# Softplus in a selective scan: the maximum and the exponential in one VectorE sum, the bias as a row of the weights, eight z buffers and seven weight buffers

## The chip, the cores and the metric

The kernel runs on one core of one Trainium2 chip. The metric is the device time of one execution in microseconds (us), as the median over several runs. All arithmetic is float32.

Engines are named as in the profile: PE is TensorE (PEld its weight loads), DVE is VectorE, ACT is ScalarE, POOL is GpSimd, SP is the queue of SyncE, which here starts nearly all DMAs. SBUF is the on-chip working memory, PSUM the accumulator memory that PE writes and that DVE and ACT can also use for other data.

## The reference, cut to what matters

The input is four images of 384 channels by 32 by 32 pixels (1024 positions). Layer 0 is a group norm followed by a selective scan in four directions, summed, normalised and passed through a GELU. Layer 1 is windowed attention over tokens and then a mixture of four experts, two per token. The change touches the time step `dt` of the scan only:

```
xs    = _cross_scan(x)                                     # 4 directions k, 384 channels d, 1024 positions l
x_dbl = einsum('bkdl,kcd->bkcl', xs, x_proj_weight)        # 44 rows: 12 for dt, 16 for B, 16 for C
dts   = einsum('bkrl,kdr->bkdl', x_dbl[:, :, :12], dt_projs_weight)
dt    = softplus(dts + dt_projs_bias[None, :, :, None])
# scan, for each of 16 states per channel:
h     = h * exp(dt * A) + (dt * u) * B
y     = sum over the states of h * C
```

So two things leave the softplus: `dt` itself, which feeds the exponentials, and the product `dt * u`, which feeds the other factor.

## The kernel before, in words

**Tiling.** A turn is one image and one direction; there are 16. A turn has three channel tiles of 128, so there are 48 time steps in the sense of `time_steps` (L741): one computes `dt` and `dt * u` for 128 channels and 1024 positions. Each time step then serves 16 scan slots: a tile of 128 partitions holds 32 channels times 4 states, so 4 blocks of channels times 4 groups of states, 768 slots in all.

**One time step** (L741 to L796). PE multiplies 12 rows of `x_dbl` (tile `xd`) by the weights `dtw_sb` into two PSUM banks of 512 positions each (`ps_dt`). ACT takes the absolute value into `e` and the ReLU into `dt`, adding the bias in both, and gives the banks back. ACT makes `e = exp(-e)` over 1024 positions. It takes two banks again (`ps_sp`, called `w` in the code), writes `w = 1 + e`; DVE computes the rounding error `e = (w - 1) - e`, ACT takes the logarithm of `w` in place, and DVE, for each half, subtracts `e`, adds `dt` (both into `w` in PSUM), and multiplies `w` by the input `u` (tile `ub`) into `e` in SBUF. ACT copies `w` into `dt` in SBUF and the bank goes back. Two DMAs write `e` and `dt` to DRAM (`dtr`), from where `spread` (L798) loads them repeated four times per channel (tiles `dtu` and `dts`).

**One slot.** POOL multiplies the spread `dt * u` by B into a z buffer (`times_b`, L808). ACT makes `dA = exp(dt * A)` in PSUM, in one of two `dA` tiles (`decay`, L824). DVE runs the recurrence (`scan`, L850) either in place in z or into `dA`. The product with C follows on POOL (`z<-z,bc`) or on DVE (`z<-dA,bc`), whichever the planner finds earlier free. PE sums the four states of each channel (`fold_y`, L884), one PSUM bank for eight slots, and then gives the z buffers back.

**Buffers.** There are `NZ = 7` z buffers of 4 KB per partition, and `NWT = 8` buffers of 4.5 KB (`wt`) for expert weights; while the attention of an image runs, four of these hold its weights. Three PSUM banks are shared by the folds, the softplus and all other work (`banks`), and one more serves the experts' output.

**What sets the order.** The kernel is written as generators, one per task. At build time `Machine.run` (L335) steps them against a table of costs (`Engine.ask`, L154) and fixes the order of the instructions of every engine: at each step the engine that can start first issues its earliest ready request, with a bias for early or late tasks. On the chip every engine and the SP queue run this order strictly in turn, each waiting for what its next instruction needs. A bank or a buffer is taken in the planner, and on the chip its next writer waits for its last reader.

**Stages.** Group norm and projection of the first image fill the first 100 us. The scan of all four images follows, with attention, routing and experts of the earlier images in the gaps. When the last slot is done, attention of the last image and the rest of the experts remain (`experts`, L1317: 19 blocks of 128 tokens per image, 76 in all). A block uses eight weight tiles, four of the first layer (`ps_hid`) and four of the second (`y_ff`).

**Start of the SP queue.** Constants are loaded first (L394 to L405, `const_load`), among them the bias `dtb_sb`; the next instruction in the queue, the first load of `x`, waits for the set-up work on DVE.

Of the kernel before, what the change touches and what calls it, by code (L numbers as in the profile page):

```python
# [11 lines left out]
F32 = mybir.dt.float32  # L12
AF = mybir.ActivationFunctionType
ALU = mybir.AluOpType
# [3 lines left out]
P = 128  # L18
B, D, HH, WW = 4, 384, 32, 32
L = HH * WW  # L20
T = D // P
HB = 512
NH = L // HB
KG, NS, R = 4, 16, 12
# [12 lines left out]
NCH, HT = HID // CH, CH // P  # L37
MB = 2 * L // P + NE - 1
NT = L // P
NROW, NHS, NWT = 10, 4, 8  # L40
EARLY, LATER = -6.0, 6.0
LEAD = 0.6
HID_RANK = 2
GELU_BIAS = EARLY
FAVOUR = 1.0
TILES, EPS, NZ = 3, 1e-5, 7
CORES = 1
NEG = -1.0e30

# [17 lines left out]
def colmajor(ap):  # L67

    return ap.rearrange("p (h w) -> p w h", w=WW)
# [307 lines left out]
def conv_attn_hybrid(  # L377
# [7 lines left out]
    nc = tc.nc  # L385
    const = ctx.enter_context(tc.tile_pool(name="const", bufs=1))
    dram = ctx.enter_context(tc.tile_pool(name="dram", bufs=2, space=bass.MemoryType.DRAM))

    def const_load(src, shape, name):
        dst = const.tile(shape, F32, name=name)  # L390
        nc.sync.dma_start(dst, src)
        return dst

    xw_sb = const_load(xw, [P, T, KG, XR], "xw_sb")  # L394
    dtb_sb = const_load(dtb, [P, KG, T], "dtb_sb")
    ds_sb = const_load(ds_, [P, KG, T], "ds_sb")
    lnw_sb = const_load(lnw, [P, T], "lnw_sb")
    lnb_sb = const_load(lnb, [P, T], "lnb_sb")
# [72 lines left out]
    banks = Stock(m, ps_b, "ps", 3, [P, HB])  # L471
# [4 lines left out]
    with tc.tile_pool(name="setup", bufs=1) as setup:  # L476
# [15 lines left out]
        for j in range(JB):  # L492
            ps = banks.now("ps_al")
# [15 lines left out]
    work = ctx.enter_context(tc.tile_pool(name="work", bufs=1))  # L509
# [42 lines left out]
    pe, act, dve, pool, sp = m.pe, m.act, m.dve, m.pool, m.sp  # L552
# [65 lines left out]
    def group_norm(b):  # L618
# [68 lines left out]
        def project(pair):  # L687
            xos = yield from zs_.take("xo", n=2)
            for h in range(NH):
                us = yield from us_.take("ux", n=2)  # L690
                uv = [us[t // NH][:, ts(t % NH, HB)] for t in range(T)]
                for t in range(T):
                    yield from sp.dma_start(uv[t], udr[b][t][:, ts(h, HB)])
                ps = yield from banks.take("ps_x", 0)
                pv = ps[: 2 * XR, :]
                mm = Calls()
                for t in range(T):
                    mm.matmul(
                        pv, xw_sb[:, t, 2 * pair : 2 * pair + 2, :].rearrange("p k r -> p (k r)"),
                        uv[t], start=t == 0, stop=t == T - 1,  # L700
                    )
                yield from pe.all(mm)
                us_.give(*us)
                yield from act.copy(xos[0][: 2 * XR, ts(h, HB)], pv)
                yield from copy(
                    xos[1][: 2 * XR, :].rearrange("r (w h) -> r h w", h=HH)[:, ts(h, HH // NH), :],
                    pv.rearrange("r (h w) -> r h w", w=WW),
                )
                banks.give(ps)
            for n in (1, 0):  # L710
                yield from sp.dma_start(xdr[b][2 * pair + n], xos[n][n * XR : (n + 1) * XR, :])
                have.add(("x", b, 2 * pair + n))
            zs_.give(*xos)

        yield from m.together([project(pair) for pair in (0, 1)], 2 if b == 0 else 1, EARLY)

    def turn_loads():
        for i, (b, k) in enumerate(turns):
            yield lambda: ("x", b, k) in have and (i == 0 or (i - 1, T - 1) in dtrs)

            xd = work.tile([32 + R, HB], F32, tag="xd", name="xd")
            dtw_sb = work.tile([32 + R, D], F32, tag="dtw", name="dtw_sb")
            for h in range(NH):
                r = slice(32 * h, 32 * h + R)
                yield from sp.dma_start(xd[r], xdr[b][k, :R, ts(h, HB)])
                yield from sp.dma_start(dtw_sb[r], dtw[:, k])
            xds[i], dtws[i] = xd, dtw_sb

    def state_rows(c):
# [11 lines left out]
    def time_steps():  # L741

        for i, (b, k) in enumerate(turns):
            for t in range(T):
                yield lambda: i in xds and ("u", b) in have and count_of["scan"] >= (i * T + t) * TS - 40
                u = yield from us_all.take("ub")
                yield from sp.dma_start(u, udr[b][t])


                e = work.tile([P, L], F32, tag="e", name="e")  # L750
                dt = work.tile([P, L], F32, tag="dt", name="dt")
                bias = dtb_sb[:, k, t : t + 1]
                pss = []
                for h in range(NH):
                    pss.append((yield from banks.take("ps_dt", 0)))
                mm = Calls()
                for h in range(NH):
                    r = slice(32 * h, 32 * h + R)
                    mm.matmul(pss[h], dtws[i][r, ts(t, P)], xds[i][r], start=True, stop=True)
                yield from pe.all(mm)  # L760
                for h, ps in enumerate(pss):
                    c = ts(h, HB)
                    yield from act.activation(e[:, c], ps, AF.Abs, bias=bias)
                    yield from act.activation(dt[:, c], ps, AF.Relu, bias=bias)
                    banks.give(ps)
                yield from act.activation(e, e, AF.Exp, scale=-1.0)

                ws = []
                for h in range(NH):
                    w = yield from banks.take("ps_sp", 0)  # L770
                    yield from act.activation(w, e[:, ts(h, HB)], AF.Identity, bias=1.0)
                    ws.append(w)
                for h, w in enumerate(ws):
                    c = ts(h, HB)
                    yield from dve.scalar_tensor_tensor(e[:, c], w, -1.0, e[:, c], ALU.add, ALU.subtract)
                for w in ws:
                    yield from act.activation(w, w, AF.Ln)
                for h, w in enumerate(ws):
                    c = ts(h, HB)
                    yield from dve.tensor_tensor(w, w, e[:, c], ALU.subtract)  # L780
                    yield from dve.tensor_tensor(w, w, dt[:, c], ALU.add)
                    if k % 2:
                        v = slice(h * (WW // NH), (h + 1) * (WW // NH))
                        yield from dve.tensor_tensor(
                            e[:, c].rearrange("p (w h) -> p w h", h=HH),
                            w.rearrange("p (w h) -> p w h", h=HH), colmajor(u)[:, v, :], ALU.mult,
                        )
                    else:
                        yield from dve.tensor_tensor(e[:, c], w, u[:, c], ALU.mult)
                    yield from act.copy(dt[:, c], w)  # L790
                    banks.give(w)
                us_all.give(u)
                dtr = dram.tile([2, P, L], F32, tag="dtr", name="dtr", bufs=4)
                yield from sp.dma_start(dtr[1], e)
                yield from sp.dma_start(dtr[0], dt)
                dtrs[i, t] = dtr  # L796
# [679 lines left out]
    with tc.manual_schedule():  # L1476
        for b in range(B):
            m.spawn(group_norm(b), EARLY)
        for gen in (turn_loads(), time_steps(), state_rows(0), state_rows(1), spread(1), spread(0)):
            m.spawn(gen, EARLY)  # L1480
        for gen in (decay(), times_b(), scan()):
            m.spawn(gen)
        m.spawn(layer1(), EARLY)
        for gen in (prepare(), mixture()):
            m.spawn(gen, LATER)
        m.run()
# [54 lines left out]
```

## Time and profile before

| what | value |
|---|---|
| median of three runs | 4074.07 us (4067.94 to 4078.49) |
| the profiled execution | 4065.49 us, of which the span of the profile is 4063.8 us |
| scan stage, first to last slot | about 100 to 3143 us |
| stage after the scan | about 3143 to 4063 us |
| DVE busy | 2878 us (71% of the span) |
| POOL busy | 2856 us (70%) |
| ACT busy | 2433 us (60%) |
| PE busy | 3015 us (74%) |
| POOL product `z<-dts,bc` | 768 times, 2358 ns |
| DVE recurrence | 768 times, 2276 to 2288 ns |
| ACT `dA` | 768 times, 1116 ns |
| ACT ReLU into `dt`, copy into `dt` | 96 times each, 687 and 584 ns |

How to read it: the shares of busy time are means over two stages with different limits, so they are read by stage. A group of instructions is written as output, arrow, inputs; `x96` is how often it ran; "idle before" is time in which its engine had nothing running just ahead of it, and the releaser is what ended that time. All operations run through a helper, so most groups carry L141 or L152, and tiles tell them apart.

### The profile page before, as it was taken

To read this page: it belongs to the slowest core of one execution; us is meant where nothing else is said; L and a number is where in the kernel's file an instruction comes from. 1 tells how busy PE (TensorE), PEld (TensorE's weight loads), DVE (VectorE), ACT (ScalarE), POOL (GpSimd) and SP (SyncE) were. 2 spreads that over 40 slices of the span, in tenths; PEclk is the share of its full clock that TensorE was granted. 3 is DMA by queue.
4 is the path that set the end of the run, shared out by engine and by line. 5 is a ranking of instruction groups with operands and counts; after the bars stand their busy time and mean duration, and the time that the engine had idled before them with its cause. 6 is when DMAs were issued, how large, how long until landed. Compare 5 with 4: busy or idle time off the path is not lost. (4 is left out here: it accounts for less than half of the span.)

```text
span 4063.8 us, 49234 instructions
## 1 busy us (share of the span) xinstructions
PE 3014.8 (74%) x15856; PEld 1854.0 (46%) x15856; DVE 2878.0 (71%) x3064; ACT 2432.7 (60%) x3979; POOL 2855.7 (70%) x1490
## 2 busy tenths in 40 slices
PE   3554455576674888677777786767799999998998
PEld 1000000043441455445454444444466788887886
DVE  2999999998889888888888889888897232101001
ACT  3554455476774798777776787877777345222221
POOL 1999989989897789999987899899997110101001
PEclk8555566577775899878877787887799999998997
DMA  5565564634345989464668795664569754998995
GB/s 200 203 250 209 217 209 151 209 109 162 114 154 184 382 315 355 164 229 140 215 209 283 268 358 195 230 197 171 190 243 337 240 170 142 345 335 295 315 317 193
DMA packets 368570, 935.11 MB, mean 230 GB/s; under 512 B 48372, under 2 KB 160120, under 8 KB 368312
## 3 DMA queue, kind: packets, MB, share of 16 engines
q1 hardware_dynamic: 360120, 906.79, 63.6%
q0 software_dynamic: 8192, 25.17, 1.8%
q8 instruction: 126, 2.06, 0.2%
q14 instruction: 132, 1.08, 0.1%
HBM read 786.39 MB, written 164.30 MB: 234 GB/s over the span
## 5 line engine op out<-in xcount | busy, mean ns | idle before, releaser
L141 POOL TENSOR_TENSOR z<-dts,bc 128x1024 f32<-128x1024 f32 x768 | 1792.2, 2358 | 177.7 <-PE ps_y L152 95.3
L141 ACT ACTIVATE dA<-dts,a 128x1024 f32<-128x1024 f32 x768 | 851.1, 1116 | 485.5 <-DVE z L141 456.6
L152 PE MATMUL ps_y<-z,fold 128*32 128x512 f32 x3072 | 734.9, 806 | 536.1 <-POOL z L141 253.6
L141 DVE TENSOR_TENSOR_SCAN dA<-dA,z 128x1024 f32<-128x1024 f32 x393 | 899.1, 2288 | 107.6 <-ACT dA L141 88.6
L141 POOL TENSOR_TENSOR z<-z,bc 128x1024 f32<-128x1024 f32 x375 | 879.6, 2356 | 102.6 <-DVE z L141 99.7
L141 DVE TENSOR_TENSOR_SCAN z<-dA,z 128x1024 f32<-128x1024 f32 x375 | 843.8, 2276 | 41.2 <-ACT dA L141 39.4
L152 PEld LDWEIGHTS ps_hid<-xbt,w_sb 128*128 128x128 f32 x5472 | 682.1, 201 | 132.5 <-issue 25.7
L152 PE MATMUL ps_hid<-xbt,w_sb 128*128 128x128 f32 x5472 | 702.0, 286 | 38.0 <-ACT dt L141 19.4
L152 PE MATMUL y_ff<-w_sb,hs 128*128 128x384 f32 x1824 | 659.7, 500 | 19.2 <-ACT hs L141 15.2
L141 ACT ACTIVATE hs<-ps_hid,bb 128x128 f32<-128x128 f32 x912 | 270.5, 366 | 457.1 <-PE ps_hid L152 351.6
L152 PEld LDWEIGHTS ps_y<-z,fold 128*32 128x32 f32 x3072 | 95.1, 123 | 971.4 <-POOL z L141 466.2
L141 ACT ACT_TABLE_LOAD x388 | 497.8, 1283 | 17.2 <-issue 3.6
L141 DVE TENSOR_TENSOR z<-dA,bc 128x1024 f32<-128x1024 f32 x393 | 479.8, 1221 | 13.0
L152 PEld LDWEIGHTS y_ff<-w_sb,hs 128*128 128x128 f32 x1824 | 331.7, 195 | 240.5 <-issue 47.5
L141 POOL DMA_INDIRECT cb<-ysdr,idx x64 | 61.7, 963 | 441.6 <-issue 281.7
L141 DVE COPY xbt<-ps_xb 128x384 f32<-128x384 f32 x39 | 21.7, 556 | 407.7 <-PE ps_xb L152 407.7
L152 POOL TENSOR_TENSOR rn<-rn,half 128x1 f32<-128x1 f32 x96 | 52.5, 547 | 265.6 <-DVE rn L152 256.2
L141 POOL DMA_INDIRECT xsdr<-tks,idx x64 | 63.9, 999 | 168.9 <-DMA xsdr<-tks,idx 119.5
L152 PE MATMUL ps_dt<-xd,dtw_sb 12*128 12x512 f32 x192 | 99.8, 856 | 45.9 <-ACT dt L141 19.2
L152 PE MATMUL ps_o<-v,pt 128*128 128x64 f32 (+1 forms) x720 | 110.1, 315 | 19.6 <-DVE tt L141 7.2
L141 ACT COPY dt<-ps_sp 128x512 f32<-128x512 f32 x96 | 56.0, 584 | 113.5 <-DVE e L141 113.2
L152 PEld LDWEIGHTS ps_o<-v,pt 128*128 128x128 f32 (+1 forms) x720 | 104.9, 227 | 29.4 <-DVE tt L141 7.7
(189 smaller groups left out, 3219.4 us busy)
## 6 DMA issues: line engine op xcount, KB each, us to landing
w_sb<-wl SPq DMA_DIRECT2D x608, 576.0 KB
dts<-dtr SPq DMA_DIRECT2D x384, 512.0 KB
bc<-xdr SPq DMA_DIRECT2D x128, 512.0 KB
ub<-udr SPq DMA_DIRECT2D x48, 512.0 KB
dtr<-e SPq DMA_DIRECT2D x48, 512.0 KB
dtr<-dt SPq DMA_DIRECT2D x48, 512.0 KB
yp<-ydr SPq DMA_DIRECT2D x96, 256.0 KB
ydr<-yp SPq DMA_DIRECT2D x96, 256.0 KB
```

The source lines that it names most:

```text
L141: return getattr(self.real, op)(*a, **k)
L152: getattr(self.real, op)(*a, **k)
```

## The change

The bias becomes a thirteenth row of the product: `xd` is one fixed tile whose rows 12 and 44 hold ones, and the weights get a row with the bias, from a copy of the bias laid out in DRAM (`dtbr`) by twelve DMAs at the start and one more DMA per half and turn. ACT's ReLU is dropped: DVE forms `dt = max(z, 0) + e` from the PSUM product z and the exponential. The sum `1 + e` is written over z in the same bank (the second taking of banks goes away), and DVE forms `e = (w - 1) - dt`, then `dt = ln(w) - e` straight into SBUF. So ACT's copy is dropped, the bank is given back after that subtraction, and the product with `u` reads `dt` from SBUF in place of `w` from PSUM. There are eight z buffers in place of seven and seven weight buffers in place of eight.

```diff
-NROW, NHS, NWT = 10, 4, 8
+NROW, NHS, NWT = 10, 4, 7
-TILES, EPS, NZ = 3, 1e-5, 7
+TILES, EPS, NZ = 3, 1e-5, 8
...
-    dtb_sb = const_load(dtb, [P, KG, T], "dtb_sb")
...
+    xd = const.tile([32 + R + 1, HB], F32, name="xd")
+    nc.vector.memset(xd, 1.0)
+    dtbr = dram.tile([KG, D], F32, name="dtbr", bufs=1)
+    for k in range(KG):
+        for t in range(T):
+            nc.sync.dma_start(dtbr[k, ts(t, P)].unsqueeze(1), dtb[:, k, t : t + 1])
...
-            xd = work.tile([32 + R, HB], F32, tag="xd", name="xd")
-            dtw_sb = work.tile([32 + R, D], F32, tag="dtw", name="dtw_sb")
+            dtw_sb = work.tile([32 + R + 1, D], F32, tag="dtw", name="dtw_sb")
...
                 yield from sp.dma_start(dtw_sb[r], dtw[:, k])
+                yield from sp.dma_start(dtw_sb[32 * h + R : 32 * h + R + 1, :], dtbr[k : k + 1, :])
...
-                    r = slice(32 * h, 32 * h + R)
+                    r = slice(32 * h, 32 * h + R + 1)
                     mm.matmul(pss[h], dtws[i][r, ts(t, P)], xds[i][r], start=True, stop=True)
                 yield from pe.all(mm)
                 for h, ps in enumerate(pss):
+                    yield from act.activation(e[:, ts(h, HB)], ps, AF.Abs)
+                yield from act.activation(e, e, AF.Exp, scale=-1.0)
+                for h, ps in enumerate(pss):
                     c = ts(h, HB)
-                    yield from act.activation(e[:, c], ps, AF.Abs, bias=bias)
-                    yield from act.activation(dt[:, c], ps, AF.Relu, bias=bias)
+                    yield from dve.scalar_tensor_tensor(dt[:, c], ps, 0.0, e[:, c], ALU.max, ALU.add)
+
+                for h, ps in enumerate(pss):
+                    yield from act.activation(ps, e[:, ts(h, HB)], AF.Identity, bias=1.0)
+                for h, ps in enumerate(pss):
+                    c = ts(h, HB)
+                    yield from dve.scalar_tensor_tensor(e[:, c], ps, -1.0, dt[:, c], ALU.add, ALU.subtract)
+                for ps in pss:
+                    yield from act.activation(ps, ps, AF.Ln)
+                for h, ps in enumerate(pss):
+                    c = ts(h, HB)
+                    yield from dve.tensor_tensor(dt[:, c], ps, e[:, c], ALU.subtract)
                     banks.give(ps)
-                yield from act.activation(e, e, AF.Exp, scale=-1.0)
-
-                ws = []
-                for h in range(NH):
-                    w = yield from banks.take("ps_sp", 0)
-                    yield from act.activation(w, e[:, ts(h, HB)], AF.Identity, bias=1.0)
-                    ws.append(w)
-                for h, w in enumerate(ws):
-                    c = ts(h, HB)
-                    yield from dve.scalar_tensor_tensor(e[:, c], w, -1.0, e[:, c], ALU.add, ALU.subtract)
-                for w in ws:
-                    yield from act.activation(w, w, AF.Ln)
-                for h, w in enumerate(ws):
-                    c = ts(h, HB)
-                    yield from dve.tensor_tensor(w, w, e[:, c], ALU.subtract)
-                    yield from dve.tensor_tensor(w, w, dt[:, c], ALU.add)
                     if k % 2:
...
-                            w.rearrange("p (w h) -> p w h", h=HH), colmajor(u)[:, v, :], ALU.mult,
+                            dt[:, c].rearrange("p (w h) -> p w h", h=HH), colmajor(u)[:, v, :], ALU.mult,
...
-                        yield from dve.tensor_tensor(e[:, c], w, u[:, c], ALU.mult)
-                    yield from act.copy(dt[:, c], w)
-                    banks.give(w)
+                        yield from dve.tensor_tensor(e[:, c], dt[:, c], u[:, c], ALU.mult)
```

More of the change, by code (lines that the diff above doesn't have):

```diff
@@ L751, in time_steps @@
                 dt = work.tile([P, L], F32, tag="dt", name="dt")
-                bias = dtb_sb[:, k, t : t + 1]
                 pss = []
```

## The prediction

> **What bounds the kernel now.** I read the page's slices first, then busy time by stage, then the waits of the scan stage engine by engine.
>
> ```profile
> PE   3554455576674888677777786767799999998998
> DVE  2999999998889888888888889888897232101001
> ACT  3554455476774798777776787877777345222221
> POOL 1999989989897789999987899899997110101001
> ```
>
> DVE and POOL are full until slice 31 and nearly empty after it, where PE is full: a scan stage, then a PE stage. With the stages cut at 100 and 3143 us (columns: window, length, then busy us and count of PE, PEld, DVE, ACT, POOL):
>
> ```profile
> 100.00:3143.00 3043.00, 2108.12 (x10322) 1129.31 (x10323) 2714.59 (x2568) 2123.51 (x3128) 2756.80 (x1348) 0.76 0.63 222
> 3143.00:4063.00 920.00, 876.12 (x5469) 712.29 (x5468) 140.97 (x446) 279.21 (x816) 87.67 (x120) 0.96 0.76 262
> ```
>
> In the scan stage POOL is busy 91%, DVE 89%, ACT and PE about 70%. POOL and DVE are too close to rank by busy time; the waits decide (waiter, what it waited for, total us, times, longest):
>
> ```profile
> DVE dA L141 <- ACT dA L141: 88.6, 68, 3.8
> DVE z L141 <- ACT dA L141: 39.4, 35, 3.6
> DVE dA L141 <- POOL z L141: 12.5, 9, 6.3
> ...
> POOL z L141 <- DVE z L141: 99.7, 44, 13.3
> POOL z L141 <- PE ps_y L152: 95.3, 50, 10.0
> ...
> ACT dA L141 <- DVE z L141: 456.6, 287, 8.5
> ACT dt L141 <- DVE e L141: 109.3, 67, 4.9
> ```
>
> DVE waits for POOL's z only 12.5 us in all, while POOL (99.7) and ACT (456.6) wait for DVE. So DVE is the engine that paces the scan. Whatever lengthens DVE's work there moves the end; ACT work there is mostly beside it.
>
> **The change part by part.** The sum is made against the profiled execution, 4065.5 us, which lies 8.6 us under the median of the runs.
>
> *DVE's operations.* Each half of a time step had four (0.678, 0.683, 0.699, 0.861 us) and has four again. Three of the new ones read one PSUM bank and one SBUF tile, like the rows `e<-ps_sp,e` (0.678) and `ps_sp<-ps_sp,e` (0.683): 96 x (0.678 - 0.699) = -2 us. The fourth, the product with `u`, now reads both inputs from SBUF, and this is the term that counts. Before:
>
> ```profile
> L141 DVE TENSOR_TENSOR e<-ps_sp,ub x96: 667/849/1073, 84.1 to 2948.9; 128x512 f32<-128x512 f32 x96
> L141 POOL TENSOR_TENSOR z<-dts,bc x768: 2327/2357/2403, 95.7 to 3131.4; 128x1024 f32<-128x1024 f32 x192
> ```
>
> *Two inputs in SBUF.* No large DVE operation before has two inputs in SBUF. The group norm has small ones (three elements a partition; minimum, median, maximum in ns):
>
> ```profile
> L141 DVE TENSOR_TENSOR g<-g x8: 165/868/2270, 24.5 to 2066.6; 128x3 f32<-128x3 f32 x8
> ...
> L141 DVE TENSOR_SCALAR g<-ps_gm x4: 122/152/160, 27.3 to 2076.0; 128x3 f32<-128x3 f32 x4
> L141 DVE SCALAR_TENSOR_TENSOR g<-g x4: 160/1198/4556, 28.4 to 2078.3; 128x3 f32<-128x3 f32 x4
> ```
>
> The neighbour with one input, from PSUM, never exceeds 0.16 us. Those with two SBUF inputs take 0.16 us in the first group norm, when POOL is quiet, and up to 2.27 and 4.56 us in the later ones. The timeline shows why (start, length):
>
> ```profile
> 2066.46 2.34 POOL L141 TENSOR_TENSOR z<-dts,bc 128x1024 f32<-128x1024 f32 x1
> 2068.77 2.33 POOL L141 TENSOR_TENSOR z<-z,bc 128x1024 f32<-128x1024 f32 x1
> 2068.86 2.27 DVE L141 TENSOR_TENSOR g<-g,mv 128x3 f32<-128x3 f32 x1
> 2071.07 2.33 POOL L141 TENSOR_TENSOR z<-dts,bc 128x1024 f32<-128x1024 f32 x1
> ```
>
> The DVE operation ends when the POOL operation ahead of it does. Counting all 15 such operations of the scan stage (12 of the group norms, 3 `ps_r<-p,r` of 1.02, 1.24 and 1.95 us): 24.1 us in all, 2.6 at the quiet durations, so 21.4 / 15 = 1.43 us extra each.
>
> The new product runs 2 x 48 = 96 times. From POOL's rows: the first of a pair meets a POOL operation half done, 2.36 / 2 x 0.906 = 1.07 us. In the built order the second follows the first with one 0.68 us subtraction between in 45 of 48 steps, so it meets a POOL operation begun when the first let go: (2.36 - 0.68) x 0.906 = 1.52. Mean 1.30, or 125 us; ends 0 (no such wait at this size) and 1.43, or 137. I take 125 as nearest to both rows. DVE idles 11% of the stage, and I let that share absorb it: 125 x 0.89 = +111 us. If that cover is gone, +125.
>
> [...]
>
> [...]
>
> *ACT.* 96 ReLUs (0.687) and 96 copies (0.584) go, 122 us of busy time. ACT does not pace, so only DVE's waits for it can shrink. Of the 128 us that DVE waits for `dA`, the ACT instruction just ahead was a softplus one in 22 us; the largest share, 45, follows the table load after the experts' GELU. DVE waits another 11 for `ps_sp`. There is a new wait too: ACT's `1 + e` overwrites the bank that DVE's maximum reads, so it waits for DVE, with the next `dA` queued behind it on ACT and the recurrence behind that. It stands in for the removed copy's wait (109.3 us on ACT, under 1 us of it seen by DVE). I take half of 33, -16 us; ends 0 and -33. The banks, held through the exponential now and released by DVE and not ACT, gate PE, which has 30% of idle time here: 0.
>
> *The eighth z buffer.* It acts on POOL's 95.3 us of waiting for folds. DVE would see its own 12.5 of waiting for z, and less waiting for folds (39.5 for `yp`) when POOL's products come sooner. I take a quarter of 95, -24 us; ends 0 and -95.
>
> *Seventh weight buffer.* In the PE stage the loads of `xb` are issued at 3892.05, 3908.16 and 3924.28: 16.1 us a block. PE waits there for `w_sb` only 5.4 us (6.7 with the weight loads), since the queue waits for a buffer, not PE for a weight. One less shortens the lead from eight to seven loads of 2 us each. But the order changes: in the built orders 35.25 of 76 blocks stand ahead of the last fold before, 34.25 in the changed kernel. One block more after the scan: +16 us; ends 0 and +32.
>
> *DMAs.* The twelve copies of the bias cost 0.43 us of SP each, like the constants; SP idles there from 6.81 to 13.57 waiting for DVE, so 5.2 us fit. Without that cover, +5. The 32 extra row loads are 0.33 us each on SP. All but the first turn's are asked for some 40 slots, about 150 us, ahead of need. At the start a `dtw_sb` load already held PE to 75.24: +2 us; ends 0 and +7. The memset of `xd` is in the same idle stretch: 0.
>
> Sum: 111 - 2 - 16 - 24 + 16 + 2 = +87, so **4152 us**.
>
> **The rivals.**
>
> *The product does not wait at this size.* The rows with the wait have three elements; nothing shows 512. Then -2 - 16 - 24 + 16 + 2 = -24: 4041. Against it: the waits follow POOL's state, not the size. Chance 0.08.
>
> *POOL paces, and the z buffer frees it: faster.* POOL is the busier, 2757 against 2715. If its waits for folds (95.3) all go and half of those for DVE (50), and POOL pays only for the products' own time, 96 x 0.86 x 0.89 = 73, the sum is 73 + 16 + 2 - 145 = -54: 4012. It decides from where more than 91 of these 195 us go. Against it: DVE's 12.5 us for POOL. Chance 0.08.
>
> *Both engines pay.* Each product also holds POOL off for its 0.86 us, 82 us, and the two delays fall one after another, with no gains: 125 + 82 + 18 = +225: 4290; with half of POOL's share, 4250. For it: POOL has only 9% of slack. Chance 0.10.
>
> *It evens out.* With half of the wait absorbed and the full ends of ACT and z's half: 62 - 2 - 33 - 48 + 18 = -3: 4063. Chance 0.06.
>
> **How the numbers follow.** The forecast has 0.68. Its own range is 4092 (103 x 0.89, ACT -33, z -48, +16: +27) to 4225 (137 + 16 + 7, no gains: +160). The range given reaches down to the even case and up to the lower half of "both pay": 4062 to 4245, leaving out the two faster rivals (0.16) and the rest of "both pay". About 0.3%, 12 us, is what a measurement of this kernel can tell from no change. Faster holds the first two rivals, 0.16; same most of the even case, 0.04; slower the rest, 0.80.
>
> **What would show it.** Right: the product `e<-dt,ub` at about 2.1 us mean, with maxima past 2.4; DVE's busy time in the scan stage up by about 120 us though its count is the same; the last slot near 3210 us, and some 42 blocks after it at 16.1 us. Wrong: the product under 1 us; DVE waiting for POOL's z; the last slot before 3143; PE waiting for `w_sb` by tens of us in the second stage, or POOL's products or gaps grown as much as DVE's.

## The result, and the profile after

The changed kernel takes 4178.69 us (median of four runs, 4170.32 to 4186.97) against 4073.76 before: a ratio of 1.0258, 95% interval 1.0234 to 1.0283, slower. The forecast was 4152, in a range of 4062 to 4245; it was worked out from the profiled execution before, 4065.5, so its +87 stands against the +105 measured between the medians. The profiled execution has a span of 4185.0 us, 121.2 more than that of before.

The stages of the changed kernel, cut at its last fold (3241.3 us). Columns: window, length, then busy us and count of PE, PEld, DVE, ACT and POOL, granted clock, DMA share, GB/s:

```profile
100.00:3241.30 3141.30, 2135.88 (x10243) 1130.96 (x10247) 2855.66 (x2579) 2009.17 (x2924) 2806.48 (x1359) 0.75 0.62 215
3241.00:4185.00 944.00, 893.11 (x5549) 724.51 (x5542) 140.85 (x447) 283.79 (x829) 79.23 (x112) 0.96 0.77 260
```

DVE executes nearly the same number of instructions in the scan stage (2579 against 2568) and is busy 141 us longer. ACT is busy 114 us less. The first POOL product starts at 112.45 us where it was 95.67, the last fold comes at 3241.3 where it was 3146.3, and what follows takes 943.7 where it took 917.5. So of the 121.2 us, 16.8 are lost before the scan, 78.2 in it and 26.2 after it.

The product with `u`, its subtraction and POOL's products, as the tiles list them (minimum, median and maximum in ns):

```profile
L141 DVE TENSOR_TENSOR dt<-ps_dt,e x96: 660/676/692, 100.5 to 3014.2; 128x512 f32<-128x512 f32 x96
L141 DVE TENSOR_TENSOR e<-dt,ub x96: 676/2117/10343, 101.2 to 3014.9; 128x512 f32<-128x512 f32 x96
L141 POOL TENSOR_TENSOR z<-dts,bc x768: 2327/2360/3253, 112.4 to 3232.0; 128x1024 f32<-128x1024 f32 x192
```

The subtraction, with one input in PSUM, has next to no spread, 0.66 to 0.69 us. The product, with both in SBUF, runs from 0.68 to 10.34 us. Its time goes with what POOL does: the 23 products during which POOL ran nothing took 0.68 to 0.69 us or 1.03 to 1.05 us, in the same two groups that the product had from PSUM, 0.67 to 0.70 and 1.00 to 1.07. So with POOL at rest the product from SBUF took neither more nor less than the product from PSUM. POOL's longest product grew from 2.40 to 3.25 us. The page's group of the product (busy us, mean ns, idle time before):

```profile
L141 DVE TENSOR_TENSOR e<-dt,ub 128x512 f32<-128x512 f32 x96 | 238.1, 2481 | 3.0
```

It was 82.6 us and 861 ns. That is 155.5 us more, above the whole increase of DVE, 141. The waits of the scan stage (total us, times, longest):

```profile
ACT dA L141 <- DVE z L141: 698.3, 371, 13.9
...
POOL z L141 <- DVE z L141: 138.7, 49, 9.4
...
DVE dA L141 <- ACT dA L141: 70.5, 40, 8.1
...
DVE z L141 <- ACT dA L141: 31.2, 30, 5.5
POOL z L141 <- PE ps_y L152: 29.5, 10, 6.9
DVE dA L141 <- POOL z L141: 24.7, 15, 3.0
```

Everybody waits for DVE more than before: ACT 698 us against 457, POOL 139 against 100. POOL's wait for folds fell from 95 to 30 us, the doing of the sizes: with the old ones it is 118 (after_sizes, below). DVE itself waits for POOL's z only 24.7 us.

### The profile page after: what moved, and what is told of

Read it like the earlier page. It is cut to its first block, busy times and chain, and to the rows that moved or that the text cites. A ratio compares the mean times of both kernels' runs of the same rounds, so it can differ in the third digit from the quotient of the medians.

```text
span 4185.0 us, 48945 instructions
## 1 busy us (share of the span) xinstructions
PE 3055.7 (73%) x15850; PEld 1867.9 (45%) x15850; DVE 3014.0 (72%) x3070; ACT 2310.7 (55%) x3769; POOL 2892.7 (69%) x1493
## 3 DMA queue, kind: packets, MB, share of 16 engines
q14 instruction: 128, 1.05, 0.1%
## 5 line engine op out<-in xcount | busy, mean ns | idle before, releaser
L141 POOL TENSOR_TENSOR z<-dts,bc 128x1024 f32<-128x1024 f32 x768 | 1814.6, 2388 | 108.9 <-DMA dts<-dtr 72.6
L152 PE MATMUL ps_y<-z,fold 128*32 128x512 f32 x3072 | 746.6, 796 | 596.4 <-POOL z L141 347.1
L141 POOL TENSOR_TENSOR z<-z,bc 128x1024 f32<-128x1024 f32 x378 | 890.7, 2366 | 151.8 <-DVE z L141 138.7
L141 DVE TENSOR_TENSOR_SCAN dA<-dA,z 128x1024 f32<-128x1024 f32 x390 | 891.7, 2286 | 95.6 <-ACT dA L141 70.5
L152 PE MATMUL y_ff<-w_sb,hs 128*128 128x384 f32 x1824 | 675.0, 509 | 21.7 <-ACT hs L141 9.5
L152 PEld LDWEIGHTS y_ff<-w_sb,hs 128*128 128x128 f32 x1824 | 336.6, 198 | 252.1 <-issue 56.1
L141 DVE TENSOR_TENSOR e<-dt,ub 128x512 f32<-128x512 f32 x96 | 238.1, 2481 | 3.0
L152 PE MATMUL ps_s<-k,q 64*128 64x192 f32 (+1 forms) x384 | 93.7, 397 | 43.6 <-DVE dt L141 12.2
L152 PE MATMUL ps_dt<-xd,dtw_sb 13*128 13x512 f32 x192 | 89.7, 826 | 43.1 <-DMA xd<-xdr 17.1
```

Of the source, the lines that this page charges most:

```text
L141: return getattr(self.real, op)(*a, **k)
L152: getattr(self.real, op)(*a, **k)
```

## The experiments

The kernels were measured in groups, each beside the kernel before, and each ratio is against its runs in the same group. Their medians were 4073.8 us beside the changed kernel, 4077.2 beside the next four rows, 4073.7 beside the four after those and 4079.0 beside the last two, so small differences between groups are better read from the ratios than from the medians. The stages come from the profiles: the scan from the first POOL product to the last fold, the rest from there to the end of the span, each of one execution; the one of psum_rows_z9w6 was its slowest, 4067.3 us. The blocks are those of the experts that stand ahead of the last fold in the built order.

| kernel | median us | ratio (95%) | first POOL product | scan us | after it us | product mean us | blocks ahead |
|---|---|---|---|---|---|---|---|
| before | 4073.8 | 1 | 95.7 | 3050.6 | 917.5 | 0.861 | 35.25 |
| changed | 4178.7 | 1.0258 (1.0234 to 1.0283) | 112.4 | 3128.9 | 943.7 | 2.481 | 34.25 |
| psum_product | 4053.8 | 0.9949 (0.9930 to 0.9968) | 111.8 | 2976.7 | 964.8 | 0.865 | 32.75 |
| before_sbuf_product | 4171.9 | 1.0243 (1.0223 to 1.0262) | 96.1 | 3162.0 | 902.4 | 2.117 | 36.75 |
| after_sizes | 4197.7 | 1.0292 (1.0269 to 1.0314) | 107.5 | 3161.3 | 927.7 | 2.331 | 35.0 |
| after_rows | 4166.1 | 1.0219 (1.0199 to 1.0239) | 98.2 | 3127.9 | 944.1 | 2.437 | 34.25 |
| wide_product | 4129.6 | 1.0131 (1.0088 to 1.0175) | 106.2 | 3066.0 | 956.3 | 4.121 (48) | 33.5 |
| before_sizes | 4063.3 | 0.9971 (0.9956 to 0.9987) | 100.3 | 3045.8 | 915.5 | 0.860 | 35.0 |
| psum_rows | 4044.0 | 0.9931 (0.9910 to 0.9952) | 97.7 | 2981.1 | 963.0 | 0.864 | 32.75 |
| psum_rows_sizes | 4058.4 | 0.9962 (0.9945 to 0.9979) | 96.0 | 3031.1 | 927.5 | 0.862 | 34.75 |
| psum_rows_z7w7 | 4077.8 | 0.9998 (0.9985 to 1.0011) | 95.6 | 2993.2 | 983.6 | 0.863 | 32.25 |
| psum_rows_z9w6 | 4053.9 | 0.9927 (0.9900 to 0.9954) | 93.9 | 2986.2 | 985.4 | 0.861 | 32.25 |

### The product from PSUM again

```diff
-                    yield from dve.tensor_tensor(dt[:, c], ps, e[:, c], ALU.subtract)
-                    banks.give(ps)
+                    yield from dve.tensor_tensor(ps, ps, e[:, c], ALU.subtract)
...
-                        yield from dve.tensor_tensor(e[:, c], dt[:, c], u[:, c], ALU.mult)
+                        yield from dve.tensor_tensor(e[:, c], ps, u[:, c], ALU.mult)
+                    yield from act.copy(dt[:, c], ps)
+                    banks.give(ps)
```

> The changed kernel with one thing undone: the last subtraction stays in PSUM, the product with u reads it from there, and ACT copies it into dt, as before the change. Theory A (a product with two inputs in SBUF waits for POOL, 2.48 us a product instead of 0.86): the product falls back to 0.86 us, 155 us of DVE time go, of which 89% shows, less some 16 us for the copies that ACT has again: 4178 - 138 + 16 = 4056, between 4030 and 4090. Theory B (the new order and the buffer sizes are what costs): the time stays within 20 us of 4178. Theory C (the loads at the start cost): it stays within 5 us of 4178 apart from what the copies add.

4053.8 us, as theory A had it, and 0.5% under the kernel before. The product is back to its old self:

```profile
L141 DVE TENSOR_TENSOR e<-ps_dt,ub x96: 681/852/1069, 100.1 to 2883.5; 128x512 f32<-128x512 f32 x96
```

The product's busy time falls by 155.1 us and the scan stage by 152.2, with ACT's copies added. The two can't be set against each other as they stand, because the planner builds another order for this form, with its copies: 1.5 blocks fewer stand ahead of the last fold. Their work leaves the scan too, DVE's whole busy time there falls by 169 us (2850 to 2681), and the stage after the scan grows by 21. The median falls by 125.

### The product from SBUF in the kernel before

```diff
-                    yield from dve.tensor_tensor(w, w, dt[:, c], ALU.add)
+                    yield from dve.tensor_tensor(dt[:, c], w, dt[:, c], ALU.add)
+                    banks.give(w)
...
-                        yield from dve.tensor_tensor(e[:, c], w, u[:, c], ALU.mult)
-                    yield from act.copy(dt[:, c], w)
-                    banks.give(w)
+                        yield from dve.tensor_tensor(e[:, c], dt[:, c], u[:, c], ALU.mult)
```

> The kernel before with one part of the change alone: the sum goes straight into dt in SBUF, the product with u reads dt, and ACT's copy goes. Bias, banks, maximum and buffer sizes are as before. Theory A: the product takes about 2.4 us, 96 x 1.5 x 0.89 = +128 us, less up to 16 us for ACT: 4074 + 112 = 4186, between 4140 and 4220. Theories B and C: no loss, 4074 or up to 16 us less.

4171.9 us: this one part makes nearly the whole loss, though it also frees ACT of its copies and returns the banks earlier. The median grows by 95. The product takes 120.6 us more and the scan stage 111.4 more; the stage after it is 15 us shorter, with 1.5 blocks more ahead in the built order, and these are part of DVE's 143 us more in the scan.

```profile
L141 DVE TENSOR_TENSOR e<-dt,ub x96: 675/1392/10515, 84.0 to 3035.2; 128x512 f32<-128x512 f32 x96
```

### The sizes and the start, each alone

```diff
-NROW, NHS, NWT = 10, 4, 7
+NROW, NHS, NWT = 10, 4, 8
-TILES, EPS, NZ = 3, 1e-5, 8
+TILES, EPS, NZ = 3, 1e-5, 7
```

> The changed kernel with seven z buffers and eight weight buffers again. Theory A: the product's wait is untouched; the eighth z buffer was worth about 24 us and the seventh weight buffer cost about 16 to 26, so 4160 to 4205. Theory B: most of the loss goes with the sizes, below 4130.

4197.7: 19 us worse than the changed kernel by the medians and 14 by the ratios, whose intervals overlap a little. So the sizes were no cause of the loss; the runs further below show that they are a gain.

```diff
-    dtbr = dram.tile([KG, D], F32, name="dtbr", bufs=1)
-    for k in range(KG):
-        for t in range(T):
-            nc.sync.dma_start(dtbr[k, ts(t, P)].unsqueeze(1), dtb[:, k, t : t + 1])
...
-                yield from sp.dma_start(dtw_sb[32 * h + R : 32 * h + R + 1, :], dtbr[k : k + 1, :])
+                yield from sp.dma_start(dtw_sb[32 * h + R : 32 * h + R + 1, :], dtb[k : k + 1, :])
...
-        "dtb": _channels(a["L0_conv_dt_projs_bias"]),
+        "dtb": a["L0_conv_dt_projs_bias"],
```

> The changed kernel with the bias handed over as rows of channels, so that the 32 row loads read it directly and the twelve copies of single elements at the start are gone. Theory C in its small form (the copies hold up the first loads of x by 11 us and the first product of POOL by 17): 4178 - 11 to 4178 - 17, 4161 to 4167, with the first POOL product near 96 to 101 us. Theory A alone, with the copies hidden as predicted: 4176 to 4178.

4166.1, 12.6 us less by the medians and 16 by the ratios, as the small form of theory C had it. The same step from psum_product to psum_rows, below, is 10 by the medians and 7 by the ratios, so leaving the copies out is worth some 10 us. The timeline of the changed kernel (start, length) shows the place:

```profile
6.39 9.97 SPq L722 DMA_DIRECT2D dtbr<-in_dtb_dram  x12
16.54 3.00 SPq L141 DMA_DIRECT2D xn<-in_x_dram  x3
20.98 4.46 SPq L141 DMA_DIRECT2D un<-in_x_dram  x3
28.18 1.29 DVE L141 BATCH_NORM_STATS2 st<-xn 128x6 f32<-128x512 f32 x2 [14.71 <-DMA xn<-in_x_dram]
```

and the same stretch without the copies:

```profile
12.65 1.28 SPq L141 DMA_DIRECT2D xn<-in_x_dram  x3
13.97 1.61 SPq L141 DMA_DIRECT2D un<-in_x_dram  x3
16.44 1.29 DVE L141 BATCH_NORM_STATS2 st<-xn 128x6 f32<-128x512 f32 x2 [3.24 <-DMA xn<-in_x_dram]
```

With the copies the loads of `x` are issued 4 us later and take 11.6 us, not 3.8, until DVE has the first of them. The first POOL product moves by 14 us. Why the loads take longer behind the copies was not tested.

### One product of 1024 in place of two of 512

```diff
-                        yield from dve.tensor_tensor(e[:, c], dt[:, c], u[:, c], ALU.mult)
+                    yield from dve.tensor_tensor(e, dt, u, ALU.mult)
```

(once a time step, after both subtractions; the same for the column order)

> The changed kernel with one product over 1024 positions a time step in place of two over 512: half as many operations with two inputs in SBUF, the same elements. If each operation pays its own wait for POOL (theory A): the second wait of a pair goes, the product's busy time falls from 238 us to about 48 x (1.6 + 1.9) = 168, and the time by 0.89 x 70 to 4116, between 4095 and 4150. If the loss is a slower reading of SBUF by the element (rival): the busy time stays at 230 to 240 and the time at 4178.

4129.6: the same elements in half as many operations give back 49 us. Busy time falls from 238 to 198 us. A slower reading by the element would have left it at 230 to 240; a wait per operation would have given 168 if the first wait of a pair were 1.6 us. That wait is longer, as the pairs of the changed kernel show: the first product of a pair takes 3.31 us on average, the second 1.65. Less 0.86, that is 2.45 and 0.79 of waiting. The wide product waits about as long as the first of a pair: 4.12 us, less 1.72 for two halves without a wait, an estimate from the 0.861 us of the product from PSUM, is 2.40. So the wait is per operation, and the second of a pair waited less than the first.

### The sizes in other surroundings

```diff
-NROW, NHS, NWT = 10, 4, 8
+NROW, NHS, NWT = 10, 4, 7
-TILES, EPS, NZ = 3, 1e-5, 7
+TILES, EPS, NZ = 3, 1e-5, 8
```

> The kernel before with eight z buffers and seven weight buffers, nothing else. The reversal of the sizes in the changed kernel cost 19 us; if they are worth the same here, 4055, between 4045 and 4066. If they are worth only what DVE waits for POOL's z (12.5 us), less one block more after the scan (16), 4074 to 4080.

0.9971: some 12 us, and 4063.3 as the median, inside the first range and well above its 4055.

The next kernels join the product from PSUM and the direct bias rows, with 8 z and 7 weight buffers, then with other numbers of these, by the same two lines.

> The changed kernel with the product read from PSUM and the bias rows read directly: both costs found so far taken out. If they add up, 4054 - 13 = 4041, between 4030 and 4052.

> The same with seven z buffers and eight weight buffers: the new form of the softplus alone, without the sizes. If the sizes are worth 19 us in every form, 4060, and the form alone 14 to 17 us against the kernel before; if the form is worth nothing, 4074.

> The product from PSUM and the direct bias rows, with seven z buffers and seven weight buffers: against the run with 7 and 8 it shows the price of the weight buffer, against the run with 8 and 7 the worth of the z buffer. In the built order 32.25 blocks of the experts stand ahead of the last fold, 34.75 with 7 and 8, 32.75 with 8 and 7. If the weight buffer costs only the blocks that move behind the scan (2.5 x 16 us) and the scan stage keeps the 3031 us it has with 7 and 8: 4058 + 40 = 4098, and the z buffer is worth some 54 us. If the weight buffer costs nothing: 4058.

> The same with nine z buffers and six weight buffers, 32.25 blocks ahead of the last fold. If a ninth z buffer shortens the scan stage as the eighth did (50 us with 12 us or so less of it left to gain) and the block moved behind costs 8 to 16: 4025 to 4044. If POOL's 32 us of waiting for folds is all that is left to gain and DVE sees little of it: 4050 to 4070.

The first is at 0.9931 and beats both kernels, 3 us above the sum of its two parts. The second is where it was expected. The third, 4077.8, lies half way between its two expectations. Nine and six, at 0.9927, cannot be told from the first: a ninth z buffer for a weight buffer brings nothing that shows. At seven weight buffers the eighth z buffer takes the ratio from 0.9998 to 0.9931, some 27 us; at seven z buffers the eighth weight buffer takes it from 0.9998 to 0.9962, some 15 us. The new form of the softplus with the old sizes and ACT's copies, 0.9962, is worth some 15 us against before. Both sizes together are worth 12 to 14 us by the ratios in all three places: in the kernel before (0.9971), in the changed kernel (1.0292 to 1.0258) and in the form with the product from PSUM (0.9962 to 0.9931).

The stages show how differently the two sizes work. Taking a weight buffer away (7 and 8 to 7 and 7) shortens the scan by 37.9 us and lengthens what follows by 56.1: fewer experts run in the gaps of the scan, 32.25 blocks instead of 34.75, and PE does them afterwards. Adding the z buffer (7 and 7 to 8 and 7) shortens the scan by 12.1 us and what follows by 20.6, with half a block more ahead. Over all the rows the second stage goes from 902 us (36.75 blocks ahead) to 984 (32.25): about 18 us a block, 82 over 4.5, if the blocks alone make the difference.

## Why the prediction was right, and where its terms were off

The direction, the cause and the size of the loss came as forecast. Some of its terms came out near by luck, and this is said with them.

**DVE paces the scan: held.** When the product went back to PSUM, DVE's busy time in the scan fell by 169 us and the stage by 152; when it was moved to SBUF in the kernel before, DVE's rose by 143 and the stage by 111.

**Two inputs in SBUF: right in kind, too small.** I priced the wait at 1.30 us a product, with 1.07 for the first and 1.52 for the second of a pair. Measured were 1.62, with 2.45 and 0.79. The term that was off is "the first meets a POOL operation half done". Of the first products 44 of 48 started while POOL was at work, about the share I had, but these waited 2.68 us on average and not 1.18. Of the second products only 28 of 48 did, not 91%; those waited 1.36 and not 1.68. So the first was priced too low and the second too high, and the mean of 1.30 lies as near to 1.62 as it does because the two errors partly cancel. The 103 in the lower end of the prediction's own range, 4092, is 1.07 us on every product; no run shows that, and the 96 products of the changed kernel waited 156 us.

Of the 72 products in all that started with POOL at work, 56 got through at the end of the POOL operation then running, as I had it. The others waited over further operations, up to a whole train, as here in the changed kernel (start, length):

```profile
1539.81 4.66 POOL L141 TENSOR_TENSOR z<-dts,bc 128x1024 f32<-128x1024 f32 x2
1541.91 10.34 DVE L141 TENSOR_TENSOR e<-dt,ub 128x512 f32<-128x512 f32 x1
1544.43 2.35 POOL L141 TENSOR_TENSOR z<-z,bc 128x1024 f32<-128x1024 f32 x1
1546.73 4.64 POOL L141 TENSOR_TENSOR z<-dts,bc 128x1024 f32<-128x1024 f32 x2
1552.17 0.68 DVE L141 TENSOR_TENSOR dt<-ps_dt,e 128x512 f32<-128x512 f32 x1
1552.88 1.05 DVE L141 TENSOR_TENSOR e<-dt,ub 128x512 f32<-128x512 f32 x1
```

POOL stops at 1551.37, the product ends 0.88 us later, and the second of the pair finds POOL idle and takes 1.05. Nearly all the long waits end in this way: in 12 of the 14 longest POOL had come to a stop before the product was done, and in 10 of these POOL's next instruction, a product `z<-z,bc`, was released by DVE's z (in the row shown PE released it last). So in most of them POOL ran on until its own order needed a result that DVE was to deliver after the product. With POOL stopped, the second product of the pair often met nothing: 20 of 48 started with POOL at rest.

The row that I had, 4.56 us for a group norm operation, already held this, and I averaged it away. In the kernel before it starts during one POOL operation and ends with the next:

```profile
1287.71 4.65 POOL L141 TENSOR_TENSOR z<-dts,bc 128x1024 f32<-128x1024 f32 x2
1287.83 4.56 DVE L141 SCALAR_TENSOR_TENSOR g<-g 128x3 f32<-128x3 f32 x1
```

The same trace had another hint that I left out. Small DVE copies with one input, from SBUF to SBUF, spread as well, the long ones with POOL at work (`g<-mv`, 0.17 to 1.63 us, and `k<-k`, 0.27 to 1.97), so operations with two inputs are not the only ones that wait.

**The absorbed 11%: not refuted, and not shown.** I let DVE's idle share hide part of the wait and gave no reason why it should. In the scan stage 152 of DVE's 169 us showed in the one run and 111 of 143 in the other, 90 and 78%; in the medians it was 125 of the product's 155 us and 95 of 121, 81 and 79%, with ACT's copies and the moved blocks in them. These runs can't tell the cover from the copies and the blocks. With the price, the term of +111 measured +125, net of ACT's copies.

**ACT, the z buffer and the block behind the scan: right in the numbers, the paths not as I had them.** I had -2, -16, -24 and +16, together -26. The form of the softplus with its copies is worth 15 us (psum_rows_sizes), the z buffer 27, the weight buffer costs 15, and all of these together make 0.9931, or -28 (psum_rows). That the z buffer's 27 is near my 24, and the weight buffer's 15 near my 16, is luck. For the z buffer the scan itself gained 12.1 us, though POOL's wait for folds fell by 34 (66.2 to 32.2); the rest came behind it, where I had nothing, half a block less and what else is open. The weight buffer moved 2.5 blocks there, not one, and its 15 us are what is left of two larger changes, 37.9 less and 56.1 more. What dropping the copies alone is worth was not run.

In the changed kernel the stage after the scan is 26.2 us longer with one block more, where I had 16. PE is busy 893 us there against 873, so 20 of it is PE's work; it waits for `w_sb` 7.2 us against 5.4.

**The DMAs at the start: wrong.** The step that failed is the price "0.43 us of SP each, like the constants" and the cover "5.2 us fit". The twelve copies of single elements held SP for 9.97 us, and the loads of `x` behind them came late: +17 in the profile where I had +2, and some 10 us of the time when they were taken out (7 to 16).

**The sum.** By the medians: product 125, start 13, and the rest by subtraction, 105 - 138 = -33, against 111, 2 and -26. The two prices that were too low make +25, the rest -7: together the 18 between 87 and 105. The other 8 or 9 us between the forecast of 4152 and the measured 4178.7 are the lower base from which it was worked out.

**The rivals.** The product does wait at this size (before_sbuf_product). POOL does not pace: its wait for folds fell by 66 us, and DVE, whose busy time grew, set the time. In the kernel before with the new sizes that wait fell by 50 us (95.3 to 45.8) and the time by 12. That both engines pay in full did not happen: POOL's products took 22 us more in `z<-dts,bc`, 2388 against 2358 ns, not 82. The gains did not make up for the wait.

**The signs.** The product's mean is 2.48 us where I had about 2.1, with maxima past 2.4 as said; DVE's busy time in the scan rose by 141 where I had about 120; the last POOL product of the scan starts at 3232 where I had the last slot near 3210.

## What to carry to other kernels

Before moving an operand of DVE from PSUM to SBUF to save a copy, see whether POOL works on SBUF at the same time, as it did here, where the product's mean went from 0.86 to 2.48 us: look in the trace for any DVE operation on SBUF alone, however small, and compare its quiet and its busy duration, and its maximum as well as its mean. The 122 us of instructions that ACT was rid of, which does not pace here, did not make up for a wait of 156 us on the engine that does. And read a stage together with the one after it: a weight buffer less made the scan 38 us shorter and the kernel 15 us longer, since the work that the scan had covered came behind it.

## What the runs showed of the hardware that I had not expected

The DVE product with two SBUF inputs waited at times for several POOL operations, not one. Of the 96 products of the changed kernel, 14 waited longer than 2.4 us, about one POOL operation, and they hold 86 of the 156 us of waiting; the longest is 10.34 us over five POOL operations, while 31 took under 1.2 us. The reverse is mild: POOL's longest `z<-dts,bc` grew by 0.85 us, about the length of one DVE product (0.86 from PSUM). The POOL operations that DVE waited for include ones that started after it, four of them in the row of 10.34 us. Why the end of a POOL operation let DVE through in 56 of 72 cases and not in the other 16 stays open.

Twelve DMAs of 128 single elements each took 0.83 us of the queue apiece, where the constants start 0.47 us apart, and the 512 KB loads behind them took 11.6 us from issue to use where they took 3.8.
